# Four residual image layers in one program: layer 0's loop issued in the order of the text, batch statistics moved into layer 2, and the scan's products in bands

## The chip, the cores and the metric

The kernel runs on one core of a Trainium2 chip. The metric is device time in microseconds (us) of one execution; three executions of the kernel before were timed, and the median is used. A core has five instruction queues that run side by side and meet through semaphores: TensorE (PE in the profile; its weight loads are listed apart as PEld), VectorE (DVE), ScalarE (ACT), GpSimd (POOL) and SyncE (SP), which here issues the DMAs. Each queue runs its instructions in the order in which they stand in it, so an instruction that waits holds up what stands behind it.

## What is computed

The input x is 16 images of 64 x 64 pixels and 256 channels in 32-bit floats. Four layers follow one another, each of the form "x plus f(group norm of x)", with 32 groups of 8 channels per image:

```python
# layer 0: linear attention, 8 heads of 32, over the 4096 pixels of an image
q, k, v = split(gn(x) @ Wqkv); q = softmax(q over 32 dims) / sqrt(32); k = softmax(k over pixels)
out = layernorm(((k^T v / 4096) applied to q) @ Wout + bout);  x = x + out
# layer 1: channel gate from mean and max per channel, then two maps of one value per pixel
xc = gn(x) * sigmoid(fc(avg) + fc(max));  m = mean over channels of xc
y  = scan over the 4096 pixels: h = exp(softplus(d*m)*A)*h + softplus(d*m)*m*B(m);  y = sum(h * C)
s  = conv7x7([mean, max over channels of xc]);  x2 = xc*sigmoid(y) + xc*sigmoid(s)
x  = x + relu(batchnorm(x2))               # statistics over all images and pixels
# layers 2 and 3: involution 3x3 and 7x7, each pixel with its own kernel made from its channels
```

Batch norm in layer 1 is the one place where all 16 images meet: its mean and variance need x2 of all of them.

## The kernel before

**Stages.** An image is cut into NCH = 8 chunks of CT = 512 pixels. Activations stand with channels on the 128 partitions, in two halves h. The program is one stage after another: layer 0 (with layer 1's channel gate and maps), layer 1's convolution and scan, layer 1's statistics, layer 2 (which first applies layer 1's end), layer 3. Between stages the activations lie in device memory (x1_d, x2_d, x3_d).

**Layer 0's loop** (from line 566) has LAST = 256 turns and 16 more at its end. An image takes 16 turns: a block of 8 turns for the first 128 output channels of q, k and v (hf = 0), then a block for the others (hf = 1). Turn n, with t = n mod 8, issues work of several stages of several images:

- `attended` projects chunk t of the current block: pq (L280) and pkv (L292) on TensorE, with copies to qa (L284) and ka, va (L301) on ScalarE. Its input xn is normalised (`normalised0`, L166 on VectorE) at the end of the turn before.
- `context` (L318 to L364) belongs to the block before: the maximum of ka by a tree (L311 to L315), a transpose pk (L331), the spreading of the maximum pb (L338), the subtraction (L341) and exponential (L344), the product pctx (L350) of exp(k) with v, and its scaling to cs (L359).
- `weighted` does the softmax of qa: maximum (L387), subtraction on POOL (L375), exponential (L380), sum (L383), reciprocal (L384) and scaling on POOL (L375).
- `output` applies cs to a part of qa: transpose qT (L405), product po (L408), transpose o (L409). PARTS gives the parts of each turn t.
- `projected0`, in the turns of hf = 1, takes the image before: py (L423), bias y (L428), squares (L432) and their sum ss (L433), the scaling of y, transposes pt (L444), yT (L448), the residual addition with maximum (L451), and the store to x1_d.
- `entered` loads the next image's chunk xin and takes statistics (L246); after the eighth, `norm0` makes mean and scale. `gate1` makes layer 1's norm and channel gate after the last projected chunk (av L469, ph L477, pgate L487, gate L491).
- `mapped` takes the image two before: affine of xm (L172, L175), transposes px (L505), and maximum and sum over channels into maps (L509, L510).

The group norms take a power -1/2 on POOL (`inv_sqrt`, L93 and L94, result gn_r). Chains such as `context` are generators: `step()` lets each run to its next yield, and a turn calls it five times (start, twice from `between`, after `entered`, after `mapped`).

In this loop the framework's scheduler decides the order of the instructions in each engine's queue, from the text, dependencies and priorities. The scan and layer 2 stand under `tc.manual_schedule()`: there each queue follows the text.

PSUM buffers set part of the order: py, pkv and px share the tag mm with two buffers, pq, pt and po the tag tr with three, and pk, pb, pctx and the small products one buffer.

**Scan.** The maps of 16 images are turned into r3, whose three kinds of values (softplus d, d*m*m, d*m) are transposed to rows (L726, pr) of 48 partitions, copied (L731), and spread with wrow to 128 partitions of (image, state) by two products pa (L736) of 48 rows each: one for the decay exponent, one for the input. After the exponential a scan instruction (L749) runs over 512 pixels; pys (L760) sums the states. There are 16 steps, 8 chunks by two groups of 8 images.

**Statistics.** For each of 128 tiles of 512 pixels, x1 is loaded (L789), the factor sigmoid(y) + sigmoid(s) is spread over partitions by a product pf (L792) with a one-hot column, VectorE multiplies and sums (L797), and ScalarE squares and sums (L801). Some 20 small VectorE operations make batch norm's scale and shift. The factor, held in SBUF as `held`, is also stored to fac_d.

**Layer 2** begins by loading its constants (17 DMAs on SP), then in each of its first 128 turns reads a tile of x1 and of the factor (`load_layer1`: two DMAs each, the factor broadcast to all partitions), makes z (L970) on VectorE, the relu (L976) on ScalarE and x2 on POOL (L980), and goes on with the involution, whose product pd stands on VectorE (L1102). Its reads of a tile are ordered by image rows: a tile takes 256 pixels from each half of the image.

Of the kernel before, what the change touches and what calls it, by code (L numbers as in the profile page):

```python
# [15 lines left out]
P = 128  # L16
C = 256
# [19 lines left out]
def network(ctx: ExitStack, tc: tile.TileContext, a: dict, out: bass.AP):  # L37
# [142 lines left out]
    with ExitStack() as st:  # L180
# [59 lines left out]
        def entered(i, ch):  # L240

            if ch == 0:
                st0[i] = wk.tile([P, 2, NCH, 6], F32, tag="st0", name="st0")
            xin = loaded.pop(("xin", i, ch))
            for h in range(2):
                nc.vector.bn_stats(st0[i][:, h, ch, :], xin[:, h])  # L246
            if i >= 2:
                stores.extend(halo.pop(0) for _ in range(min(3, len(halo))))
            if ch == NCH - 1:
                chains.append(norm0(i))  # L250
# [8 lines left out]
        normal = {}  # L259

# [57 lines left out]
        def context(i, hf):  # L318
# [4 lines left out]
            t = tree_max(  # L323
                lambda t: [kf[:, 8 * k : 8 * k + 8, :] for k in range(4)]
                + [t.rearrange("p (j e) -> p j e", e=P)],
                lambda t: [(t[:, 0:n], t[:, n : 2 * n]) for n in (512, 256, 128)],
            )
            yield
            yield
            pk = sm.tile([P, CT], F32, tag="sm", name="pk")  # L330
            nc.tensor.transpose(pk[:, 0:P], t[:, 0:P], ident)  # L331
            kmc = small.tile([P, 1], F32, tag="kmc", name="kmc")
            nc.vector.tensor_reduce(kmc, pk[:, 0:P], AX.X, ALU.max)
            diag = wk.tile([P, P], F32, tag="diag", name="diag")
            nc.vector.tensor_scalar(diag, ident, kmc, None, ALU.mult)
            yield
            pb = sm.tile([P, CT], F32, tag="sm", name="pb")
            nc.tensor.matmul(pb[:, 0:P], lhsT=ones, rhs=diag, start=True, stop=True)  # L338
            for jh in range(2):
                part = kf[:, jh * 16 : (jh + 1) * 16, :]  # L340
                nc.vector.tensor_tensor(  # L341
                    part, part, pb[:, 0:P].unsqueeze(1).broadcast_to([P, 16, P]), ALU.subtract
                )
                nc.scalar.activation(part, part, AF.Exp)  # L344
            yield
            yield
            pctx = sm.tile([P, CT], F32, tag="sm", name="pctx")
            for j in range(32):
                for h in range(4):
                    nc.tensor.matmul(  # L350
                        pctx[32 * h : 32 * h + 32, 0 : NB + 1],
                        lhsT=ka[:, j, :, h], rhs=va[:, j, :, h],
                        start=(j == 0), stop=(j == 31),
                    )
            rz = small.tile([P, 1], F32, tag="rz", name="rz")
            nc.vector.reciprocal(rz, pctx[:, NB : NB + 1])

            cs = wk.tile([P, P], F32, tag="cs", name="cs")
            nc.vector.scalar_tensor_tensor(  # L359
                cs.rearrange("p (h e) -> p h e", h=4),  # L360
                pctx[:, 0:NB].unsqueeze(1).broadcast_to([P, 4, NB]), rz,
                hmask.rearrange("p (h e) -> p h e", h=4), ALU.mult, ALU.mult,
            )
            ctx_m[i, hf] = cs  # L364

        def weighted(i, hf):
# [11 lines left out]

            def exponential(k):
# [6 lines left out]
            for k in range(2):  # L386
                nc.vector.tensor_reduce(mq[:, halves[k]], qa[:, halves[k]], AX.X, ALU.max)  # L387
                scaled(k, mq, ALU.subtract)
                yield
            exponential(0)  # L390
            yield
            summed(0)
            exponential(1)
            yield
            scaled(0, mq, ALU.mult)
            summed(1)
            yield
            scaled(1, mq, ALU.mult)
            om[i, hf] = slots.tile([P, P, NB], F32, tag="slot", name="o")
# [13 lines left out]
        def projected0(i, ch):  # L413
# [45 lines left out]
            if ch == NCH - 1:  # L459
                chains.append(gate1(i))  # L460
# [37 lines left out]
        def mapped(i, ch):  # L498

            xc = loaded.pop(("xm", i, ch))  # L500
            affine(xc, xc, i)
            px = mm.tile([P, 4, C], F32, tag="mm", name="px")
# [14 lines left out]
        def jobs(n):  # L517
# [18 lines left out]
            if at(i - 2) and (t >= 2 if hf == 0 else t < 2):  # L536
                todo.append(("xm", i - 2, (t - 2) % NCH))
            if 12 <= d < 16:
# [5 lines left out]
        PARTS = ((), (), (), (0,), (1,), (2, 3), (4, 5), (6, 7))  # L544
        PARTS_LAST = ((), (), (), (0, 1), (2, 3, 4), (5, 6, 7), (), ())

        def loads(n):
            for job in jobs(n):
                if job[0] == "q":
                    load("xn", job[1], job[3])  # L550
                else:
                    load(*job)

        for ch in range(NCH):
# [4 lines left out]
            stores.clear()  # L559
        while chains:  # L560
# [3 lines left out]
        projecting = []  # L564
        for n in range(LAST + 16):
# [5 lines left out]
            loads(n + 1)  # L571
            if t == 0 and 0 <= before[0] < NI:
                chains.append(context(*before))
            if t == 1 and 0 <= before[0] < NI:
                chains.append(weighted(*before))
# [10 lines left out]
            for p in parts[:1]:  # L586
# [6 lines left out]
            def between(dp):  # L593
                step()
                if dp == 0:
                    for p in parts:
                        if p is not parts[0]:
                            next(p)
                    for p in parts:
# [3 lines left out]
                    for p in projecting:  # L603
                        next(p)

# [5 lines left out]
            for job in jobs(n + 1):  # L611
                if job[0] == "q":
                    normalised0(*job[1:])
# [3 lines left out]
            for job in work:  # L617
                if job[0] == "xm":
                    mapped(*job[1:])
            step()  # L620
            if t == NCH - 1 and 0 <= before[0] < NI:
                del qkv[before], ctx_m[before]
                if m >= 3 and m % 2:
                    for k in range(2):
                        om.pop((m // 2 - 1, k), None)

# [4 lines left out]
    with ExitStack() as st:  # L631
# [4 lines left out]
        sm = st.enter_context(tc.tile_pool(name="s_sm", bufs=2, space=PSUM))  # L636

# [6 lines left out]
        bng = sconst("bng", [P, 2], a["bn_gamma"])  # L644
        bnb = sconst("bnb", [P, 2], a["bn_beta"])
# [4 lines left out]
        wrow = sconst("wrow", [3 * NI, NG, 2, P], a["wrow"].rearrange("k (g n s) -> k g n s", g=NG, n=2))  # L650
        wout = sconst("wout", [P, 16], a["wstate"])
        mv2 = sconst("mv2", [P, 2, 2, NI])
# [56 lines left out]
        r3 = sconst("r3", [P, NB, NI, 3])  # L709
        rd, rdmm, rdm = (r3[:, :, :, k].rearrange("p d i -> p i d") for k in range(3))  # L710
        nc.vector.scalar_tensor_tensor(rd, z, 0.0, az, ALU.max, ALU.add)
        nc.vector.tensor_tensor(rdm, rd, m, ALU.mult)
        nc.vector.tensor_tensor(rdmm, rdm, m, ALU.mult)
# [5 lines left out]
        with tc.manual_schedule():  # L719
# [3 lines left out]
            def rowed(ch):  # L723
                pr = tr.tile([P, CT], F32, tag="tr", name="pr")
                for q in range(4):
                    nc.tensor.transpose(  # L726
                        pr[0 : 3 * NI, q * P : (q + 1) * P],
                        r3[:, ch * 4 + q].rearrange("p i k -> p (i k)"), ident,
                    )
                rows[ch] = wk.tile([3 * NI, CT], F32, tag="rows", name="rows", bufs=2)  # L730
                nc.scalar.copy(rows[ch], pr[0 : 3 * NI, :])  # L731

            def decayed(ch, g):
                pa = mm.tile([P, 2, CT], F32, tag="mm", name="pa")
                for k in range(2):
                    nc.tensor.matmul(  # L736
                        pa[:, k], lhsT=wrow[:, g, k, :], rhs=rows[ch], start=True, stop=True
# [42 lines left out]
        facr = fac_d.rearrange("(i c) t -> i (c t)", i=NI)  # L780
# [3 lines left out]
        tot = sconst("tot", [P, 2, 2, NI, NCH])  # L784
        for i in range(NI):
            for ch in range(NCH):
                tk = slice(ch * CT, (ch + 1) * CT)
# [870 lines left out]
```

## Time and profile before

| | |
|---|---|
| median of three executions | 8218.75 us (8206.47 to 8226.33) |
| profiled execution, its own time | 8218.71 us |
| span in its trace | 8216.8 us |
| mean granted TensorE clock | 0.918 |
| layer 0 filling, 0 to 220 | 220 us |
| layer 0's steady loop, 220 to 2880 | 2660 us |
| end of layer 0's loop, 2880 to 3056 | 176 us |
| convolution and scan, 3056 to 3176 | 120 us |
| statistics, 3176 to 3409 | 233 us |
| layer 2's first turns, 3409 to 3554 | 145 us |
| layer 2, 3554 to 5854 | 2300 us |
| layer 3, 5854 to 8217 | 2363 us |

The stages follow one another, so the time is their sum, and a change is worth what it takes from the engine that ends last in its own stage. A busy time is the time in which an engine executed something, summed over the stretch. A row of waits gives the engine and line that waited, the engine, tile and line whose work ended the wait, the total in us, the number of times and the longest. In a row of the timeline, the start, the duration of the group, the engine, the line, the operation with output and inputs, shapes and count follow one another, and in brackets the idle time before it with the work that ended it.

### The profile page before, as it was taken

The numbers are of one execution on the slowest core, as the hardware profiler recorded it, in microseconds if no ns is written. First come the engines' busy times: TensorE is split into PE (matmuls) and PEld (weight loads), VectorE is DVE, ScalarE is ACT, GpSimd is POOL, SyncE is SP. The second block draws the span as 40 slices with busy tenths as digits, with TensorE's granted clock in tenths as the row PEclk, the third lists the DMA queues.
The fourth block names the chain that finished last, engine by engine and source line by source line (L and its number), as shares of the span: only waits on it lengthen the run. The fifth ranks groups of instructions, "written<-read, shape, count | busy, mean of one in ns | idle before, by whom it ended". The sixth has DMA issues, their size and how long they took to land. (4 is left out here: it accounts for less than half of the span.)

```text
span 8216.8 us, 213294 instructions
## 1 busy us (share of the span) xinstructions
PE 6831.6 (83%) x88348; PEld 5191.9 (63%) x88348; DVE 5933.2 (72%) x7071; ACT 4827.7 (59%) x11136; POOL 3044.1 (37%) x2154
## 2 busy tenths in 40 slices
PE   7888888888888867478888888888588888888897
PEld 5666666666666643156666666666477777777776
DVE  6787778787777775679999999999644444444444
ACT  3555555555555544676776767665455555555554
POOL 1222222222222210167888888887411212111112
PEclk9999999999999977798888888888799999999999
DMA  7644444344333334766777777775588888888887
GB/s 225 188 142 138 139 136 141 131 145 144 124 113 118 116 102 151 249 221 231 268 262 261 271 252 267 262 258 200 176 257 258 259 258 256 261 259 257 255 256 245
DMA packets 1079706, 1695.53 MB, mean 206 GB/s; under 512 B 136785, under 2 KB 682914, under 8 KB 1077586
## 3 DMA queue, kind: packets, MB, share of 16 engines
q1 hardware_dynamic: 1078738, 1681.89, 63.1%
q8 instruction: 696, 11.40, 0.6%
q14 instruction: 272, 2.23, 0.1%
HBM read 1234.54 MB, written 469.76 MB: 207 GB/s over the span
## 5 line engine op out<-in xcount | busy, mean ns | idle before, releaser
L1102 DVE TENSOR_TENSOR pd<-xs,pw 128x4608 f32<-128x4608 f32 x256 | 1261.2, 4946 | 1.4 <-ACT xs L1083 1.4
L1376 PE MATMUL pk<-rt,span 64*128 64x176 f32 x12288 | 1177.9, 328 | 52.6 <-issue 47.9
L1386 ACT ACTIVATE wm<-pk,spanb 128x176 f32<-128x176 f32 x2560 | 845.7, 424 | 573.4 <-PE pk L1376 570.3
L1115 POOL TENSOR_TENSOR pd<-pd 128x2048 f32<-128x2048 f32 (+2 forms) x384 | 1071.6, 2791 | 173.1 <-DVE pd L1102 82.7
L1462 POOL TENSOR_TENSOR ex<-ex,rx 128x192 f32<-128x192 f32 (+2 forms) x768 | 436.6, 570 | 1820.6 <-DVE ex L1455 1232.1
L1376 PEld LDWEIGHTS pk<-rt,span 64*128 64x128 f32 x12288 | 967.8, 191 | 132.8 <-issue 75.9
L1455 DVE SCALAR_TENSOR_TENSOR ex<-pa,msk,ex 128x192 f32<-128x192 f32 x704 | 294.3, 418 | 1006.5 <-ACT ex L1454 948.4
L292 PE MATMUL pkv<-wq,xn 128*128 128x256 f32 x4096 | 967.9, 382 | 14.4 <-ACT va L301 14.2
L1442 PE MATMUL pa<-wm,xw 126*32 126x48 f32 x45056 | 758.2, 214 | 220.9 <-issue 206.2
L375 POOL TENSOR_TENSOR qa<-qa,mq 128x1024 f32<-128x1024 f32 x256 | 507.4, 2005 | 1168.8 <-DVE mq L384 503.0
L1079 PE MATMUL pt<-ident,pad 128*128 128x128 f32 x4608 | 760.1, 327 | 214.8 <-ACT xs L1083 207.6
L1391 DVE TENSOR_TENSOR wm<-pk,spanb 128x704 f32<-128x704 f32 x896 | 794.2, 888 | 188.9 <-PE pk L1376 186.3
L292 PEld LDWEIGHTS pkv<-wq,xn 128*128 128x128 f32 x4096 | 771.3, 192 | 227.4 <-issue 101.1
L1442 PEld LDWEIGHTS pa<-wm,xw 126*32 126x32 f32 x45056 | 624.6, 111 | 403.1 <-issue 359.0
L1079 PEld LDWEIGHTS pt<-ident,pad 128*128 128x128 f32 x4608 | 623.6, 168 | 401.4 <-ACT xs L1083 265.5
L1083 ACT COPY xs<-pt 128x512 f32<-128x512 f32 x1152 | 608.0, 587 | 170.1 <-PE pt L1079 167.2
L1273 DVE TENSOR_REDUCE x<-pd 128x512 f32<-128x4608 f32 x128 | 634.0, 4953 | 4.4
L280 PE MATMUL pq<-xn,wq 128*128 128x512 f32 x1024 | 528.2, 631 | 91.2 <-DVE xn L166 74.0
L423 PE MATMUL py<-wo,o 128*128 128x256 f32 x2048 | 525.0, 412 | 31.4 <-DVE maps L510 27.6
L1454 ACT ACTIVATE ex<-pa,msk 128x192 f32<-128x192 f32 x704 | 299.2, 425 | 392.7 <-PE pa L1442 198.5
L423 PEld LDWEIGHTS py<-wo,o 128*128 128x128 f32 x2048 | 487.7, 310 | 63.9 <-issue 38.0
L1033 PE MATMUL px<-x2p,wis 128*128 128x512 f32 x1024 | 467.7, 599 | 12.8 <-DMA x2p<-x_d 8.1
(234 smaller groups left out, 11663.8 us busy)
## 6 DMA issues: line engine op xcount, KB each, us to landing
xw<-strips SPq DMA_DIRECT2D x1408, 256.0 KB
xn<-in_x SPq DMA_DIRECT2D x256, 512.0 KB
x_d<-x SPq DMA_DIRECT2D x256, 512.0 KB
strips<-cen SPq DMA_DIRECT2D x352, 256.0 KB
xin<-in_x SPq DMA_DIRECT2D x128, 512.0 KB
x<-in_x SPq DMA_DIRECT2D x128, 512.0 KB
xm<-x_d SPq DMA_DIRECT2D x128, 512.0 KB
x<-x_d SPq DMA_DIRECT2D x128, 512.0 KB
```

The lines of the kernel that those rows point to most:

```text
L280: nc.tensor.matmul(pq, lhsT=wq[:, h, f0 : f0 + P], rhs=xn[:, h], start=(h == 0), stop=(h == 1),)
L292: nc.tensor.matmul(pkv[:, q], lhsT=xn[:, h, q * P : (q + 1) * P], rhs=wq[:, h, f0 + P : f0 + 384], start=(h == 0), stop=(h == 1),)
L423: nc.tensor.matmul(py[:, q, :], lhsT=om[i, hf][:, :, ch * 4 + q], rhs=wo[:, hf, :], start=(hf == 0), stop=(hf == 1),)
L1079: nc.tensor.transpose(pt[:, k, h * P : (h + 1) * P], lines[:, h, rc * 4 + e + k, 2 * j : 2 * j + P], ident,)
L1083: nc.scalar.copy(xs[:, e : e + 2, j, :], pt)
L1102: nc.vector.tensor_tensor(pd.rearrange("p r (g f) k -> p r g f k", f=16), run, pw.rearrange("p r (g k) -> p r g k", k=9).unsqueeze(3).broa ...
L1115: nc.gpsimd.tensor_tensor(pd[..., 0:n], pd[..., 0:n], pd[..., n : 2 * n], ALU.add)
L1273: nc.vector.tensor_reduce(x3[:, :, P:C], pd1, AX.X, ALU.add)
L1376: nc.tensor.matmul(pkv[:, b, m], lhsT=span[half, first + gg, s0 : s0 + P], rhs=rto[half, o // 4 * 2 + m, :], start=True, stop=True,)
L1386: nc.scalar.activation(dst[:, m // 2, m % 2], pkv[:, m // 2, m % 2], AF.Identity, bias=spanb[:, g0 + m : g0 + m + 1],)
L1391: nc.vector.tensor_tensor(dst, pkv, spanb[:, g0 : g0 + 4].rearrange("p (b m) -> p b m", b=2).unsqueeze(3).broadcast_to([P, 2, 2, NTL]), AL ...
L1442: nc.tensor.matmul(pav[p0 : p0 + 32, :, tj * TC : (tj + 1) * TC].rearrange("c g (w v) -> c g w v", v=2), lhsT=xw[0:TILE_IN, k, tj, 32 * q ...
```

## The change

**Layer 0's loop** comes under `tc.manual_schedule()`, so every queue follows the text, and the text is rearranged. `context` and `weighted` become lists of links, each run at a given step after the chain's start, by the tables CONTEXT and WEIGHTED (a turn has five steps). The chains `norm0` and `gate1` wait in a list `waiting` until turn t = 1 of the next block. PARTS moves to turns 4 to 7, two parts each. The qT of all parts of a turn stands at its start. xn is normalised in `between(0)` and no longer at the end of the turn. The transposes px and the maps come a turn after the affine of xm. x1 is loaded in its own turn and not a turn ahead. xm of the last image but one is taken in turns 2 to 5 behind the last block.

**Statistics** move to the start of layer 2's section, as `batch_norm()`. Images 1 to 15 come first, in 120 tiles; image 0 comes last, in layer 2's own tiles, whose x1 and product z stay in SBUF, so that layer 2's first eight turns load neither x1 nor the factor and make no z. Loads run five tiles ahead in six buffers (four buffers before). `held` is read back from fac_d, behind the constants on SP.

**Scan.** r3 is laid out in bands of 32 partitions: per group of 8 images, one band for d and one for d*m*m and d*m. It is set to zero by POOL first, and filled by six operations and not three. The products pa read 8 and 16 rows at partitions 64g and 64g + 32 instead of 48 rows each.

```diff
@@ layer 0
-                chains.append(norm0(i))
+                waiting.append(norm0(i))
+        def until(links):
+            at = 1
+            for step_no, link in links:
+                while at < step_no:
+                    yield
+                    at += 1
+                link()
-        def context(i, hf):
+        def context(i, hf, at):
...
+            links = [maximum, diagonal, spread] + [
+                lambda jh=jh: exponential(jh) for jh in range(2)
+            ] + [product]
+            return until(zip(at, links))
-        def weighted(i, hf):
+        def weighted(i, hf, at):
...
+            links = []
+            for f in (shifted, exponential, summed, lambda k: scaled(k, mq, ALU.mult)):
+                links += [lambda f=f, k=k: f(k) for k in range(2)]
+            order = sorted(range(8), key=lambda n: at[n])
+            return until([(at[n], links[n]) for n in order] + [(max(at), ended)])
-                chains.append(gate1(i))
+                (waiting if i < NI - 1 else chains).append(gate1(i))
@@ mapped
             affine(xc, xc, i)
+            yield
             px = mm.tile([P, 4, C], F32, tag="mm", name="px")
@@ jobs
-            if at(i - 2) and (t >= 2 if hf == 0 else t < 2):
+            if at(i - 2) and d < 0 and (t >= 2 if hf == 0 else t < 2):
                 todo.append(("xm", i - 2, (t - 2) % NCH))
+            if 2 <= d < 6:
+                todo += [("xm", NI - 2, 2 * d - 4 + k) for k in range(2)]
-        PARTS = ((), (), (), (0,), (1,), (2, 3), (4, 5), (6, 7))
+        PARTS = ((), (), (), (), (0, 1), (2, 3), (4, 5), (6, 7))
+        CONTEXT, CONTEXT_LAST = (1, 5, 14, 14, 15, 19), (1, 3, 4, 4, 4, 7)
+        WEIGHTED, WEIGHTED_LAST = (1, 3, 5, 7, 11, 13, 12, 14), (1, 2, 3, 4, 4, 5, 5, 6)
@@ the loop
+        in_order.enter_context(tc.manual_schedule())
         for n in range(LAST + 16):
...
             loads(n + 1)
+            for job in jobs(n):
+                if job[0] == "x1":
+                    load(*job)
...
+            if t == 1:
+                chains.extend(waiting)
+                waiting.clear()
...
-            for p in parts[:1]:
+            for p in parts:
                 next(p)
             def between(dp):
                 step()
                 if dp == 0:
-                    for p in parts:
-                        if p is not parts[0]:
-                            next(p)
                     for p in parts:
                         next(p, None)
                     for p in old:
                         next(p, None)
                     for p in projecting:
                         next(p)
+                    for job in jobs(n + 1):
+                        if job[0] == "q":
+                            normalised0(*job[1:])
+                    for p in mapping:
+                        next(p, None)
+                    mapping.clear()
...
-            for job in jobs(n + 1):
-                if job[0] == "q":
-                    normalised0(*job[1:])
...
-                    mapped(*job[1:])
+                    mapping.append(mapped(*job[1:]))
+                    next(mapping[-1])
@@ scan
+        r3 = pc.tile([P, NB, 2, 2, 32], F32, tag="r3", name="r3")
+        nc.gpsimd.memset(r3, 0.0)
...
+                    p0 = 64 * g + 32 * k
+                    band = slice(p0, p0 + 8 + 8 * k)
                     nc.tensor.matmul(
-                        pa[:, k], lhsT=wrow[:, g, k, :], rhs=rows[ch], start=True, stop=True
+                        pa[:, k], lhsT=wrow[band], rhs=rows[ch][band], start=True, stop=True
                     )
@@ statistics, now in layer 2
+            nc.sync.dma_start(out=held, in_=fac_d)
+            todo = [(i, ch) for i in range(1, NI) for ch in range(NCH)]
+            todo += [(0, rc) for rc in range(NCH)]
...
+            for k in range(5):
+                begin(k)
+            for k, (i, ch) in enumerate(todo):
+                begin(k + 5)
...
+                for h in range(2):
+                    z = x1[:, h] if i else kept[ch][1][:, h]
+                    at = slice(i * NCH + ch, i * NCH + ch + 1)
+                    nc.vector.scalar_tensor_tensor(
+                        z, x1[:, h], ngm1[:, i, h : h + 1], pf, ALU.add, ALU.mult,
+                        accum_out=tot[:, 0, h, at],
+                    )
+                    sq = z if i else wk.tile([P, CT], F32, tag="sq", name="sq", bufs=1)
+                    nc.scalar.activation(sq, z, AF.Square, accum_out=tot[:, 1, h, at])
@@ layer 2
+            if i:
                 x1, pf = taken("x1"), taken("pf")
...
+            else:
+                x1, zs = (t.rearrange("p h (g t) -> p h g t", g=2) for t in kept.pop(rc))
-            if end:
+            if end and end[0]:
                 load_layer1(*end)
         with tc.manual_schedule():
+            batch_norm()
             loads(0)
```

## Prediction, made before the changed kernel ran

> **What bounds the kernel now.** I read the page's totals, then a table by stage, then one image of layer 0 by blocks, then the waits of TensorE there, then single instructions.
>
> ```profile
> span 8216.8 us, 213294 instructions
> PE 6831.6 (83%) x88348; PEld 5191.9 (63%) x88348; DVE 5933.2 (72%) x7071; ACT 4827.7 (59%) x11136; POOL 3044.1 (37%) x2154
> ```
>
> No engine bounds the whole. The stages, in order: layer 0 filling, its steady loop, its tail, the scan, the statistics, layer 2's start (two rows):
>
> ```profile
> 220.00:2880.00 2660.00, 2314.36 (x16536) 1769.76 (x16535) 2050.61 (x3038) 1539.43 (x2853) 602.06 (x404) 0.95 0.42 137
> 2880.00:3056.00 176.00, 103.38 (x675) 80.85 (x674) 138.82 (x223) 71.94 (x159) 26.71 (x19) 0.72 0.35 116
> 3056.00:3176.00 120.00, 106.76 (x250) 55.76 (x251) 36.11 (x74) 22.26 (x33) 0.00 (x0) 0.54 0.01 2
> 3176.00:3409.00 233.00, 154.94 (x255) 40.81 (x253) 181.29 (x515) 176.87 (x512) 0.00 (x0) 0.93 0.85 280
> 3409.00:3468.00 59.00, 0.00 (x0) 0.00 (x0) 18.38 (x46) 24.29 (x60) 28.74 (x19) 0.50 0.68 186
> 3468.00:3554.00 86.00, 48.54 (x152) 23.92 (x152) 28.98 (x57) 59.34 (x140) 33.80 (x28) 0.79 0.87 293
> ```
>
> Columns: length, then busy PE, PEld, DVE, ACT, POOL, clock, DMA share, GB/s. The reader sees a loop with PE at 87% and DVE at 77%, a scan on PE, statistics and a layer 2 start fed by DMA (0.85, 0.87). Layers 2 and 3 behind 3554 are untouched. The loop holds 231 copies of qa (L284) at 16 per image, so 14.4 images of 184.3 us, of which PE works 160 and DVE 142. One image is two blocks of eight turns; its first rows are the second half of the channels (head, tail), then the first half of the next image (head with one tail turn, three tail turns):
>
> ```profile
> 1317.50:1371.50 54.00, 47.57 (x442) 40.11 (x443) 41.66 (x50) 34.10 (x71) 16.16 (x11) 0.94 0.30 99
> 1371.50:1417.60 46.10, 45.02 (x191) 35.28 (x191) 29.26 (x51) 31.24 (x73) 5.88 (x6) 1.00 0.43 137
> 1417.60:1475.20 57.60, 41.30 (x412) 30.02 (x412) 51.69 (x89) 29.15 (x37) 15.87 (x11) 0.91 0.45 146
> 1475.20:1499.00 23.80, 23.48 (x98) 16.01 (x97) 19.45 (x26) 11.23 (x15) 1.71 (x1) 1.00 0.59 201
> ```
>
> Tails are TensorE's (98%). In the heads it waits, in the third row for a VectorE that is 90% busy. What it waits for in the loop:
>
> ```profile
> PE pq L280 <- DVE xn L166: 74.0, 29, 5.0
> PE pk L331 <- DVE mx L315: 71.5, 28, 3.5
> PE pctx L350 <- DVE isq L93: 45.7, 14, 3.5
> PE py L423 <- DVE maps L510: 25.6, 13, 3.1
> PE px L505 <- ACT xm L172: 24.9, 13, 2.3
> ```
>
> Of 346 us in which PE idles there, these are 241.7, all at places the change moves.
>
> **The loop.** It drops no arithmetic: the same instructions stand in the order of the text, so only waits change. I walked the new order through one image, turn by turn, with durations of the trace.
>
> Second half of the channels, head (54.0). In turn 0 the tree maximum (1.21 + 1.21 + 0.68 + 0.36 + up to 1.99 = 5.3 us of VectorE) stands ahead of y, which frees the PSUM buffer that px and then the second half of pkv need: +3.0. In turn 2 the group norm's chain, now begun in turn 1 behind the softmax's shift, asks POOL for gn_r, and POOL is in two qa subtractions; gn_b waits on VectorE with everything behind it:
>
> ```profile
> 1440.21 3.78 POOL L375 TENSOR_TENSOR qa<-qa,mq 128x1024 f32<-128x1024 f32 x2 [16.07 <-DVE mq L384]
> 1450.86 0.69 POOL L94 TENSOR_TENSOR gn_r<-isq,mhalf 128x2 f32<-128x2 f32 x1 [2.21 <-DVE isq L93]
> ```
>
> That is 3.8 + 0.7 = +4.5. In the text ss (L433) comes straight behind y (L428), with ScalarE's square between, and the x1 addition behind yT:
>
> ```profile
> 1365.48 1.22 DVE L428 TENSOR_TENSOR y<-py,bout 128x1024 f32<-128x1024 f32 x1
> 1369.66 0.17 DVE L433 TENSOR_SCALAR ss<-ss 128x4 f32<-128x4 f32 x1 [2.96 <-ACT sq L432]
> ```
>
> The ss stall is there already; a yT stall in the head is new, +3.4. One output part moves from turn 3 to turn 4, -1.6. The head becomes 63.3. Tail (46.1): PE's 45.0 with small waits are 45.3, and pq waits for xn once, +1.6: 46.9. Block 100.1 -> 110.2.
>
> First half of the channels (57.6 + 23.8 = 81.4). A tail turn is now a chain on VectorE and TensorE (qT, po, o, xn, maps, statistics, affine): 8.15 us against 23.8/3 = 7.9, four of them 32.6. The first four turns lose the pk and pctx waits (71.5/28 = 2.6 and 45.7/14 = 3.3), since diagonal, exponentials and product stand turns apart; PE has 41.3 - 7.8 = 33.5 there, plus 2.0 for xn behind the maximum, plus 8.0 where ph waits for av, av for gn_r, and gn_r on POOL for four qa operations, plus 1.0: 44.5, and 2.4 for VectorE held up beside POOL. Block 79.5.
>
> On that hold-up a rule stands against the trace. The affine of xm (L175) takes 0.55 us alone and 2.14 beside POOL's qa; xn (L166) 0.46 to 0.55 alone, 0.69 on average. The Trainium skill, "SBUF — State Buffer", section "SBUF: two separate sides", calls the shared ports an exclusive lock held for the whole instruction. By it each of 16 qa operations per image (256 of 2.0 us in the span) could stop VectorE fully, 32 us; by the rows, a mean excess of 0.15 to 0.2 on 16 xn, about 3. The rows decide: both orders issue the same 256, and POOL in turns 1 and 2 finds other VectorE work half the time. I take 2.4.
>
> New image 189.7, this one 181.5, the mean one 184.3. This image was shorter than the mean, so I take the gap to the mean, +5: 14.4 x 5 = **+70**. Both ends: below, -97 (four tenths of the 241.7, rival 1); above, +130 (9 per image, if every ss stall of 2.96 also lands on a head).
>
> Costed at nothing: x1's load in its own turn, because the tile is needed only behind yT, some 9 us later (a late one would add its landing to the addition, as the 2.0 us waits of x on yT do today); maps a turn later, nothing reads them before the scan, though px then holds its PSUM buffer in the next turn (counted above); xm of the last image but one in turns 2 to 5 behind the last, inside a tail where VectorE is 79% busy: tail of the loop 0, between -20 and +20. Every load and store stays on SP's queue, which is free half the time (DMA share 0.42).
>
> **The scan.** Two steps and their transposes repeat every 12.65 us on PE, of which pa takes two times 3.78:
>
> ```profile
> 3085.44 3.78 PE L736 MATMUL pa<-rows,wrow 48*128 48x512 f32 x4
> 3089.15 1.89 PE L760 MATMUL pys<-wout,hst 128*128 128x16 f32 x8
> 3090.88 1.03 PE L726 MATMUL pr<-ident,r 128*48 128x128 f32 x4
> ```
>
> The bands put a step's two products in different row groups and PSUM banks. Layer 3's 64-row products (L1376) run 24 in 1.99 us, 0.083 each against 0.217 for a full-height product of 256 columns: about 1.8 times denser. So 3.71 -> 2.05 over 16 steps: -26; none of it if they do not overlap. The rule against it: the Trainium skill, "TensorEngine Tiling (Array Packing)", "Key Properties", has a change of tiling mode drain the array. The nearest row is the weight load of pa at L1442, 359.0 us in 783 waits, 0.46 each: 32 changes would cost +15. But this scan already alternates 48-row and 128-row products, and pys starts at 3089.15 when pa ends at 3089.22. I take 0 for drains and -25. The POOL memset of r3 (about 3.5 us, half of the 7.6 us that twice its size costs elsewhere) lies under the convolution; POOL is idle in this stage. Three DVE operations become six of half size: +0.5, forgotten. The rows copy on 128 partitions costs what 48 do.
>
> **The statistics.** In layer 2's section they stand behind its 17 constant DMAs on SP, which ran from 3413.1 to 3423.3 (10.2 us), and behind a reload of held: first product 14.3 us behind the store against 2.2: +12. The last eight tiles come in 1 KB runs: +4, by 224 against 288 GB/s. Six buffers instead of four: a tile takes 1.82 us, VectorE and ScalarE need 1.34, but DMA is at 0.85: between 0 and -10, I take 0. Kept tiles save layer 2's first eight turns their x1 and pf loads and z. The z of these turns wait for pf's DMA:
>
> ```profile
> 3416.82 0.75 DVE L970 SCALAR_TENSOR_TENSOR z<-x,ngm,pf 128x512 f32<-128x512 f32 x1 [2.63 <-DMA pf<-fac_d]
> 3429.84 0.75 DVE L970 SCALAR_TENSOR_TENSOR z<-x,ngm,pf 128x512 f32<-128x512 f32 x1 [4.21 <-DMA pf<-fac_d]
> ```
>
> From 3409 to 3468 eight turns take 59 us; at ScalarE's pace of 3.5 per turn plus the 5.1 us of batch norm they take about 35: -25, or nothing if x3 and the weights that turn 8 loads are then late. Together **-9**.
>
> **Sum.** +70 - 25 - 9 = +36 against the profiled 8218.71, which is the median of the runs shown (8218.75): **8255**. This kernel's runs let about 0.2%, 16 us, be told from no change.
>
> **Rivals.** (1) Faster. Spreading context over turns takes four tenths of the 241.7 us of PE waits without new ones, -97: 8218.7 - 97 - 34 = 8088, some 8090. For it: PE has 24 us of idle per image and DVE 42, and each moved piece is named in the waits; a POOL that finishes early removes my 4.5 and 8.0. Against: VectorE at 90% in the first-half head, and a strict order has no way round a stall. With -34 from the rest it decides below a period of 185.5 us per image. (2) The side parts give nothing: bands drain or do not overlap, turn 8 of layer 2 waits for its loads. 8219 + 70 = 8289, 8290. For it: the clock of 0.54 in the scan, and DMA at 0.87 right behind. Against: L1376. (3) The change doesn't act, because the loop is held by matrix work that no order shortens: PE's 160 of 184 in a steady chain; then -34 alone, 8185.
>
> **How the numbers follow.** The walk (8220 to 8330 with the side parts as costed) has 0.46, rival 1 has 0.30, rival 2 has 0.15, rival 3 has 0.09. Faster is rival 1, half of rival 3 and a little of the walk's lower edge: 0.37; same 0.07; slower 0.56. The range reaches from rival 1's middle to the walk with +120: 8080 to 8340. The walk alone: 8220 to 8330.
>
> **What would show it.** In the profile after: loop period 187 to 192; POOL named as releaser of gn_b and av; ss waiting on sq in every y turn; pk and pctx waits gone from PE; pa pairs starting together and a scan cycle near 9.4 us; no pf loads in eight turns. The forecast is wrong if the period is under 185.5, or if ss and gn_r stalls fall where PE has its own work.

## The result, and the profile after

The changed kernel takes 8255.89 us (median of four, 8253.33 to 8262.13) against 8220.52 us of the kernel before: 1.0046 times as long, with a 95% interval from 1.0032 to 1.0059. It is slower by 35 us, and the forecast was 8255. The agreement within a microsecond is partly luck: the loop with its tail and the statistics were each off by more than 50 us, in opposite directions. The stages show that. Their rows in the trace after, with the columns as before (length, busy PE, PEld, DVE, ACT, POOL, clock, DMA share, GB/s), are the steady loop, its tail, convolution and scan, the wait for held, the statistics, and layer 2's start:

```profile
220.00:2994.00 2774.00, 2343.90 (x16499) 1770.06 (x16498) 2022.13 (x3063) 1548.67 (x2833) 590.13 (x405) 0.95 0.41 137
2994.00:3197.00 203.00, 106.60 (x674) 85.02 (x674) 150.46 (x241) 73.59 (x161) 29.85 (x20) 0.70 0.28 95
3197.00:3287.00 90.00, 78.15 (x248) 45.83 (x247) 30.56 (x58) 22.21 (x33) 0.00 (x0) 0.56 0.00 0
3287.00:3302.00 15.00, 0.03 (x1) 0.06 (x1) 1.92 (x8) 0.01 (x1) 8.12 (x2) 0.50 0.31 77
3302.00:3476.00 174.00, 145.42 (x272) 42.30 (x272) 169.13 (x503) 168.16 (x501) 0.00 (x0) 0.98 1.04 384
3476.00:3598.00 122.00, 48.07 (x153) 24.30 (x152) 36.46 (x91) 86.98 (x212) 54.38 (x45) 0.71 0.75 242
```

To compare stages, the same events are taken in both traces: the last pq, the first product of the convolution (psc), the store of held, the first pd of layer 2, the first pk of layer 3, and the end of the span.

| stage, between events | before | after | difference | forecast |
|---|---|---|---|---|
| loop, to the last pq | 2884.7 | 2998.2 | +113.5 | +70 |
| tail, to the convolution | 174.7 | 198.5 | +23.8 | 0 |
| convolution and scan, to held's store | 115.0 | 90.3 | -24.7 | -25 |
| statistics and layer 2's start, to pd | 379.3 | 310.7 | -68.6 | -9 |
| layer 2 | 2371.4 | 2371.5 | +0.1 | 0 |
| layer 3 | 2291.7 | 2282.3 | -9.4 | 0 |
| sum | | | +34.7 | +36 |

Layer 3's code is the same in all kernels of this study, and its time from the first pk to the end lay between 2268 and 2306 us in fourteen traces. So -9.4 is no effect. The start of the convolution scatters too: with the loop of before it lay at 3059.4, 3069.3 and 3072.1 in three traces, with the changed loop at 3196.7 and 3204.3. A difference of some 10 us between two single traces shows nothing.

By the two rows of the steady loop (2660.00 us before, 2774.00 after), TensorE is idle in it for 430 us against 346, and busy for 2344 against 2314 on the same products. So some 84 of the 114 us more are waits, and 30 are longer work, as far as modelled matmul ends tell; why the work is longer was not tried.

Of the five waits of TensorE that were read before, pk's and pctx's are gone, and those of pq for xn and of py for maps are halved; px's wait for xm rose from 24.9 to 37.0, and others stand beside it. TensorE's waits in the changed kernel from 220 to 3000 us (engine, line, releaser: total us, times, longest):

```profile
PE ph L498 <- DVE av L490: 99.4, 14, 7.1
PE py L444 <- ACT va L311: 86.7, 42, 4.8
PE px L527 <- ACT xm L172: 37.0, 14, 2.8
PE px L527 <- DVE y L449: 34.6, 13, 2.7
PE pq L290 <- DVE xn L166: 33.9, 29, 1.6
...
PE pt L465 <- ACT qa L294: 22.0, 15, 2.4
```

VectorE's waits in the same stretch, its first line and two further down:

```profile
DVE ss L454 <- ACT sq L453: 260.2, 118, 2.3
...
DVE gn_b L255 <- POOL gn_r L94: 62.7, 14, 4.5
DVE av L490 <- POOL gn_r L94: 36.4, 14, 4.3
```

And the longest of ScalarE's:

```profile
ACT sq L453 <- DVE y L449: 450.3, 118, 7.4
```

The same waits before, from 220 to 2880 us, by the lines of that kernel:

```profile
PE pkv L292 <- ACT va L301: 14.2, 19, 1.3
PE py L423 <- ACT va L301: 2.6, 1, 2.6
...
DVE ss L433 <- ACT sq L432: 179.2, 62, 3.0
...
DVE gn_b L255 <- POOL gn_r L94: 4.7, 14, 0.8
...
ACT sq L432 <- DVE y L428: 123.2, 94, 6.3
```

pk no longer waits for the maximum, and pctx no longer for isq. Instead ph (the channel gate) waits 7.1 us in every image, py waits for the copies of va, and gn_b waits 62.7/14 = 4.5 us. How one leads to the next is seen in one turn of a head of the changed kernel. The timeline of VectorE:

```profile
1399.31 0.16 DVE L255 TENSOR_TENSOR gn_b<-gn_m,gn_r 128x2 f32<-128x2 f32 x1 [4.48 <-POOL gn_r L94]
...
1400.04 1.22 DVE L449 TENSOR_TENSOR y<-py,bout 128x1024 f32<-128x1024 f32 x1
```

That of ScalarE:

```profile
1401.29 0.42 ACT L453 ACTIVATE sq<-y 128x256 f32<-128x256 f32 x1 [6.85 <-DVE y L449]
...
1404.15 1.90 ACT L407 ACTIVATE qa<-qa 128x2048 f32<-128x2048 f32 x1
...
1408.45 0.60 ACT L311 COPY va<-pkv 128x512 f32<-128x512 f32 x1
```

And that of TensorE:

```profile
1401.31 1.09 PE L527 MATMUL px<-ident,xm 128*128 128x128 f32 x8 [2.66 <-DVE y L449]
...
1409.10 5.75 PE L444 MATMUL py<-wo,o 128*128 128x256 f32 x16 [4.75 <-ACT va L311]
```

A tiny operation of two columns waits 4.48 us for POOL. Behind it on VectorE stands y. Behind y, on ScalarE, stand the squares (idle 6.85), and behind them the copy of qa, an exponential of 1.90, yT, xn, and last the copies of ka and va. The next py needs the PSUM buffer that va's copy frees, so TensorE stands still for 2.66 at px and 4.75 at py. In strict queues one late 2-column operation crosses four engines. This is one turn: what each link costs over the whole loop is tested below, and py's wait for va proves to be mostly another matter.

The statistics went the other way. Before, the DMA moved 280 GB/s at a share of 0.85; in the changed kernel's row above it is 384 GB/s at 1.04, and VectorE is busy 169 of 174 us. A share that passes 1 is no measure of how near a ceiling the DMA is.

### The profile page after: what moved, and what is told of

The parts are those of the page before. It is cut to its first block, busy times and chain, and to the rows that moved or that the text cites. A ratio compares the mean times of both kernels' runs of the same rounds, so it can differ in the third digit from the quotient of the medians.

```text
span 8251.5 us, 212941 instructions
## 1 busy us (share of the span) xinstructions
PE 6832.6 (83%) x88364; PEld 5201.1 (63%) x88364; DVE 5865.2 (71%) x7058; ACT 4836.9 (59%) x11136; POOL 3029.6 (37%) x2155
## 4 chain that ended last, share of the span: by engine, by line
PE 44%; DVE 32%; issue 9%; ACT 7%; DMA 5%; POOL 2%; SPq 1%; DVEq 0%; POOLq 0%; ACTq 0%
PE pk L1480 12%; DVE pd L1205 9%; PE pa L1546 8%; DVE x L1377 5%; PE pkv L302 5%; PE pq L290 3%; PE py L444 3%; PE po L429 2%; ACT sq L453 2%; PE pt L1182 2%; PE pr L1447 2%; DVE x L472 2%; DVE mq L403 2%; PE px L1136 1%; POOL qa L398 1%
## 5 line engine op out<-in xcount | busy, mean ns | idle before, releaser
L302 PE MATMUL pkv<-wq,xn 128*128 128x256 f32 x4096 | 994.1, 387 | 0.0
L456 POOL TENSOR_TENSOR rsy<-ss,mhalf 128x4 f32<-128x4 f32 x128 | 132.6, 1036 | 1501.2 <-DVE ss L454 1500.9
L444 PE MATMUL py<-wo,o 128*128 128x256 f32 x2048 | 522.9, 412 | 106.3 <-ACT va L311 86.7
```

The lines of the kernel that those rows point to most:

```text
L302: nc.tensor.matmul(pkv[:, q], lhsT=xn[:, h, q * P : (q + 1) * P], rhs=wq[:, h, f0 + P : f0 + 384], start=(h == 0), stop=(h == 1),)
L444: nc.tensor.matmul(py[:, q, :], lhsT=om[i, hf][:, :, ch * 4 + q], rhs=wo[:, hf, :], start=(hf == 0), stop=(hf == 1),)
```

## The experiments

Each ratio is to the kernel before on the same chip in the same set of runs, with a 95% interval; the changed kernel is 1.0046. The event times are from the profile of each run.

**The side parts alone, and the loop alone.** The first has the diff's parts for scan and statistics, the second its parts for layer 0.

> The loop of before with the statistics in layer 2 and the bands. Theory A, stages add up: before minus 24.7 (scan, 115.0 to 90.3 in the two traces) minus 68.6 (from the store of held to layer 2's first pd, 379.3 to 310.7) minus some 9 in layer 3: 8118 to 8128. Theory B, the gain behind the loop hangs on the new loop (which leaves other data in place, or another clock): less than half of it, above 8165.

> The new loop with the scan and the statistics of before. Theory A: before plus 113 (last pq at 2998 instead of 2885) plus 24 (from there to the convolution), so 8350 to 8360. Theory B: the loop's loss is partly an effect of the other parts, below 8320.

Measured: 8145.78 us, 0.9900 (0.9885 to 0.9914), and 8372.48 us, 1.0174 (1.0156 to 1.0192). On that chip the kernel before takes 8231.35, so the parts are -86 and +141, together +55 where the change as a whole is +35 (1.0032 to 1.0059 of 8220, +26 to +48). The intervals of the two parts are 12 and 15 us wide to each side, so the 20 us between are at the edge of what these runs can tell; within that, the stages add up. The side parts gain a little less than the 91 to 101 us of theory A, and far more than half of it. A kernel with the old loop and the new side parts is faster than the kernel before and the changed one. In its trace the side parts measure 90.5 us from psc to the store and 308.0 from there to pd, as in the changed kernel.

**The order alone.** The changed kernel without the strict order: the text stays rearranged.

```diff
-        in_order = st.enter_context(ExitStack())
-        in_order.enter_context(tc.manual_schedule())
...
-        in_order.close()
```

> The changed kernel, but the scheduler orders the queues of layer 0's loop again; the text stays rearranged. Theory A, the strict order is what costs: last pq back at 2885 within 25, total 8110 to 8150. Theory B, the rearranged text costs (parts two by two, maps a turn later, pieces of context and softmax spread): last pq stays near 2998, total 8230 to 8260. Between: both.

Measured: 8103.20 us, 0.9850 (0.9832 to 0.9867). The last pq is at 2868.3 and the convolution starts at 3026.8, 170 us sooner than in the changed kernel and 33 to 45 sooner than with the loop of before. This is theory A, and more: the rearranged text is no loss, and under the scheduler it is worth some 41 us against the side parts alone (0.9850 against 0.9900). TensorE's largest waits for the steady loop there are far from those of the strict order:

```profile
PE px L527 <- DVE y L449: 58.6, 28, 3.2
...
PE ph L498 <- DVE av L490: 35.9, 13, 2.9
PE pk L344 <- DVE mx L325: 31.8, 15, 4.3
PE py L444 <- ACT va L311: 22.7, 17, 1.5
```

**Six buffers in the statistics.** The kernel before with one number changed.

```diff
-                x1 = wk.tile([P, 2, CT], F32, tag="x1", name="x1", bufs=4)
+                x1 = wk.tile([P, 2, CT], F32, tag="x1", name="x1", bufs=6)
```

> The kernel before with one number changed: six buffers for x1 in the statistics instead of four. Theory A, four buffers leave the DMA waiting for a free buffer: a tile goes from 1.80 us to 1.34 to 1.40, 51 to 59 less, total 8160 to 8170. Theory B, 280 GB/s is what the DMA gives there and the gain in the changed kernel came from the hand order or the layout of tiles: within 15 of before.

Measured: 8174.66 us, 0.9931 (0.9911 to 0.9952), -57. One number in the old kernel gives what the statistics' steady part gives in the changed one. From first to last pf it is 177.6 us for 128 tiles, 1.40 each, against 230.1 before. The stage of this run:

```profile
3184.00:3363.00 179.00, 147.33 (x256) 39.30 (x256) 172.53 (x509) 171.64 (x508) 0.00 (x0) 0.97 0.99 360
```

VectorE now is busy 172.5 of 179 us; the DMA was not at its end before, it waited for a free buffer. Three rows of waits, the first two of the kernel before (3176 to 3409 us; SPq is SyncE's queue, where the loads are issued), the third of this run:

```profile
SPq L789 <- ACT x L801: 170.9, 124, 3.9
DVE x L797 <- DMA x<-x_d: 33.5, 57, 1.8
...
DVE x L797 <- DMA x<-x_d: 2.2, 3, 1.1
```

Before, nearly every load was held at its issue until ScalarE's square had freed a buffer. With six buffers SyncE's queue still waits there (118.2 us), but two loads further ahead, and VectorE hardly waits for data.

**Where the strict order loses: three cuts of the chain.** Four kernels, all in strict order. The first puts the yield ahead of the squares, the second delays the subtractions on POOL, the third has these two edits together, and the fourth starts the norm chains where they are made.

```diff
@@ squares later
             nc.vector.tensor_tensor(y, py, bout.unsqueeze(1).broadcast_to([P, 4, C]), ALU.add)
+            yield
...
             nc.gpsimd.tensor_tensor(rsy, ss, mhalf, ALU.pow)
             yield
-            yield
@@ shift later
-        WEIGHTED, WEIGHTED_LAST = (1, 3, 5, 7, 11, 13, 12, 14), (1, 2, 3, 4, 4, 5, 5, 6)
+        WEIGHTED, WEIGHTED_LAST = (5, 7, 8, 9, 11, 13, 12, 14), (1, 2, 3, 4, 4, 5, 5, 6)
@@ norms at once
-                waiting.append(norm0(i))
+                chains.append(norm0(i))
...
-                (waiting if i < NI - 1 else chains).append(gate1(i))
+                chains.append(gate1(i))
```

> The changed kernel with the squares of y, their sum and the power issued one step later, behind the copy of qa and the transposes of o, and no longer straight behind y. In the changed kernel ScalarE stands 450 us in front of the squares waiting for y, with the copies of qa, ka and va queued behind, and TensorE loses 86.7 us on py waiting for va and 34.6 on px waiting for y; VectorE loses 260 us on ss. Theory A, this chain (y, squares, copies, PSUM buffer, py) is a large part of what the strict order costs: 60 to 110 us faster than the changed kernel. Theory B, the group norms behind POOL are the whole of it and the head's other waits take over: less than 25 faster.

> The changed kernel with one table changed: the softmax's two subtractions on POOL stand four steps later (steps 5 and 7, exponentials at 8 and 9), so that the group norms of turn 1 find POOL free. In the changed kernel TensorE loses 99.4 us on ph waiting for av, and VectorE 62.7 and 36.4 on gn_r. Theory A, POOL's queue is what costs: these three waits fall under 25 each and the kernel gains 50 to 90. Theory B, turn 1 and 2 of a head are full on VectorE anyway, and the wait moves to the subtraction's own users: less than 20 gained, or a loss.

> Both of these edits together. If the two stalls lie one after another on the path, the gains add, and the strict order comes to within 40 of the version that the scheduler orders (8103 in the last runs). If each only uncovers the other, or a third limit (VectorE's 90% in the first-half head), the sum is under six tenths of the two gains.

> The changed kernel with the group norm chains started where they are made, at the end of a block, and not held until turn 1. They then meet TensorE's tail and the maximum of turn 0, and POOL is free of subtractions. Theory A (POOL's queue costs): ph's wait for av falls under 40, 40 to 90 gained. Theory B (the chain costs wherever it stands in a strict order, since VectorE waits at gn_b and av in front of everything else): ph, gn_b and av keep over 100 us of the 198 together, less than 20 gained.

Measured, and the start of the convolution in each trace:

| kernel | us | ratio (interval) | psc starts |
|---|---|---|---|
| changed kernel | 8255.89 | 1.0046 (1.0032 to 1.0059) | 3196.7 |
| squares later | 8157.90 | 0.9937 (0.9916 to 0.9957) | 3103.5 |
| shift later | 8171.71 | 0.9951 (0.9933 to 0.9969) | 3124.8 |
| both | 8197.88 | 0.9979 (0.9969 to 0.9990) | 3145.9 |
| norms at once | 8135.81 | 0.9907 (0.9891 to 0.9924) | 3081.0 |

Each single cut gains 72 to 116 us at the convolution's start. POOL's queue is a cause: with the shift later, VectorE's two waits for gn_r fall from 62.7 to 10.5 and from 36.4 to 0.7, and ph's from 99.4 to 39.0 (under 25 was expected). The gain of 78 us is in theory A's range, though waits for ScalarE grow: pt's for the scaling of y from 15.7 to 89.6, and px's for xm from 37.0 to 63.2. From TensorE's waits with the shift later:

```profile
PE pt L465 <- ACT y L460: 89.6, 16, 6.1
PE py L444 <- ACT va L311: 67.9, 42, 2.2
...
PE px L527 <- ACT xm L172: 63.2, 14, 5.0
PE ph L498 <- DVE av L490: 39.0, 14, 4.2
```

With the norms at once, ph's wait for av and gn_b's for gn_r are not in the lists at all, and VectorE's wait of av for gn_r falls from 36.4 to 10.0: theory A, with a larger gain than its 40 to 90. TensorE's largest waits are now these:

```profile
PE pg L134 <- DVE gn_mv L107: 80.4, 27, 3.3
PE py L444 <- ACT va L311: 73.0, 42, 2.9
PE pq L290 <- ACT xn L165: 35.2, 14, 2.5
```

So py's wait for va (86.7) hangs only in small part on the late norm: it is still 73.0 where gn_b's wait is gone, and 67.9 where it is small.

The squares' place is a cause of its own: ph keeps its 99.4, and 93 us are gained all the same. VectorE's wait at ss falls from 260.2 to 30.8, but the wait at o rises from 88.9 to 242.6, so most of VectorE's idle time only moved. On TensorE, px's wait for y falls from 34.6 to 13.5, py's for va from 86.7 to 68.9, and pt's for qa (22.0) is gone; these are places that ScalarE's copies or y release. From TensorE's waits with the squares later:

```profile
PE py L444 <- ACT va L311: 68.9, 42, 3.4
...
PE px L527 <- DVE y L449: 13.5, 8, 1.7
```

The two edits together gain 51 us at the convolution's start, far under six tenths of the two gains (93 and 72) and less than either, so they do not add; against the shift alone this is at the edge of the intervals. TensorE's waits are not where the sum is lost. In the steady loop it is idle for 370 us with the squares later and for 375 with both, but busy for 2324 and 2359, at a granted clock of 0.96 and 0.94 (the first row is the squares', the second that of both):

```profile
220.00:2914.00 2694.00, 2323.88 (x16517) 1766.65 (x16516) 2015.08 (x3069) 1552.27 (x2842) 604.81 (x405) 0.96 0.42 141
...
220.00:2954.00 2734.00, 2359.09 (x16471) 1797.45 (x16470) 2040.08 (x3054) 1544.87 (x2824) 617.05 (x404) 0.94 0.41 139
```

So 35 of the 40 us between these two are longer work on the same products at a lower clock. It is so in every timed run: over the whole kernel the clock was 0.914 to 0.920 in 16 runs with both edits, and 0.920 to 0.924 in four with the squares alone. What lowered it was not tried.

**Norms at once, with the squares, and with the scheduler.**

> In the strict order, with the norm chains at once and the squares one step later: the two edits that gained 112 and 88 against the changed kernel. Theory A, they take different stalls from the path: at least 150 together, some 0.978 of before, which would beat the scheduled version (0.985). Theory B, as with the squares and the later shift, each edit makes VectorE wait at the transposes of o or the x1 addition in place of the stall removed: no better than the norms alone (0.991).

> The scheduler's order on the new text, with the norm chains at once. If a scheduled queue has gone round POOL already (ph's wait for av is 35.9 us there, not 99.4), this edit is worth little: within 20 of the scheduled version (0.985). If the place in the text counts as much as in the strict order, 60 or more better.

Measured: in strict order with both, 8114.18 us, 0.9888 (0.9867 to 0.9909), 13 us sooner at the convolution than with the norms alone (0.9907), which neither the times nor the traces can tell from nothing. That is theory B: the best strict order tried is still slower than the scheduler's on the same text with the norms held back (0.9850). py's wait for va is 92.1 there (22.7 under the scheduler with the norms held), so this cost of the strict order remains, and what sets it was not found.

With the scheduler and the norms at once: 8020.53 us, 0.9768 (0.9742 to 0.9794), some 67 us better than with the norms held (0.9850), and 52 us at the convolution's start. By the time this is the second expectation, but its reason holds by half only: the same edit gave 116 us at the convolution's start in strict order. The products of the convolution in the trace of the run with the scheduler and the norms at once (line, engine, operation and count, then shortest, median and longest ns, then first and last start in us):

```profile
L727 PE MATMUL psc<-maps,convT x20: 590/601/1190, 2975.0 to 2986.2; 128*128 128x512 f32 x20
```

And in the trace of the strict order with the norms at once:

```profile
L730 PE MATMUL psc<-maps,convT x20: 590/602/1190, 3081.0 to 3090.9; 128*128 128x512 f32 x20
```

| convolution starts at | scheduler | strict order |
|---|---|---|
| norms at once | 2975.0 | 3081.0 |
| norms held until turn 1 | 3026.8 | 3196.7 |
| text of before (norms at once) | 3059.4 | |

So the loop's +137 can be told as three parts, each to some 10 us: the rest of the rearranged text -84, holding the norms +52 under the scheduler, and the strict order +170 on top. The parts hang on the order in which they are taken: with the norms at once the strict order costs 106, and holding the norms costs 116 in strict order. The strict order on the old text was not tried.

**The constants on another queue.** Layer 2's constants are issued from ScalarE's queue, held and the first tiles alone from SP; with the scheduler, and then with the norms at once as well.

```diff
-                nc.sync.dma_start(out=t, in_=src)
+                nc.scalar.dma_start(out=t, in_=src)
```

> The scheduled version with layer 2's 17 constant DMAs issued from ScalarE's queue, so that held and the first x1 tiles are not behind them on SP. In the changed kernel held's load is issued 11.9 us after its store, and the first product 14.9 after. If SP's queue is that wait: product 5 to 7 us after the store, 8 to 10 us less. If the store's own landing and the release of buffers set it: no change there.

> The scheduled order, norm chains at once, and layer 2's constants from ScalarE's queue. The two gains lie in different stages, so they add: 0.9768 less 0.0012 to 0.0015, about 0.9755. If the constants' gain was noise of two chips, 0.9768.

Measured: 8068.21 us, 0.9835 (0.9812 to 0.9858) and 8017.25 us, 0.9763 (0.9738 to 0.9789). Neither can be told from the run without the edit by its time. In the traces the first product of the statistics comes 4.9 to 5.8 us behind the store, not 15.0 to 15.5, so SP's queue was the wait. But from the store to pd it is 304.9 against 310.8, and 307.8 against 310.0 with the norms at once: only 2 to 6 us of the 10 are kept. The tiles then take 179 us from first to last pf, not 173 to 174, most likely because they start while the constants still load (184 to 257 GB/s in the second to fourth of 40 slices of the statistics with the norms held, 202 to 234 with the norms at once, and 370 to 408 in most later ones). The last kernel is the fastest of the study by its median, and not distinguishable from the one with SP's constants.

## Why the prediction was right

The direction, the size of the sum and the place of the loss were forecast: slower, in layer 0's loop, by the waits of a strict order, with the side parts giving part of it back. Its steps:

- The stall of gn_b behind POOL was put at 4.5 us per image and measured 62.7/14 = 4.5; ph behind av and four qa operations was put at 8.0 and measured 7.1. The delayed norm chain is shown as a cause by the norms at once: -116 us at the convolution.
- The step of the loop that was mis-sized is the period: 184.3 + 5 = 189 us per image forecast, 2774/(230/16) = 193.0 measured, just outside the 187 to 192 that was to show it. The walk had py's wait for va at nothing: 86.7/14.4 = 6.0 us per image, where pkv and py together waited 1.2 before. It had y's delay free px's buffer late, and stopped there; ss waiting for the squares was named, but as a cost on VectorE alone, and the run with the squares later shows costs of it on TensorE. Neither the norms nor the squares explain most of py's wait (73.0 and 68.9 without each, 92.1 without both). The walk also kept TensorE's work at 160 us per image, which measured 2344/14.4 = 163.
- Image against image, the walk itself gave 189.7 - 181.5 = +8.2, near the measured +8.7. The step to +5 sets a walked image, made from a short one, against the mean image; this took a third of the difference away (and 14.4 x 5 is 72, not 70). Since the walk lacked the terms above, its +8.2 is luck as well. The steps of the tree maximum add up to 5.45 us, not 5.3; nothing hangs on it.
- On VectorE beside POOL, the walk set the lock that it quotes against the rows. Where an operation meets a POOL operation they agree: here xn begins 0.36 us behind the first of two POOL operations of some 2.0 us, and ends 0.2 us behind it, having taken 1.85 us in place of 0.55. Both rows are of the kernel before:

```profile
1347.96 1.85 DVE L166 TENSOR_SCALAR xn<-xn,gn_m,gn_r 128x512 f32<-128x512 f32 x1 [0.50 <-DMA xn<-in_x]
...
1347.60 3.98 POOL L375 TENSOR_TENSOR qa<-qa,mq 128x1024 f32<-128x1024 f32 x2 [11.69 <-DVE mq L384]
```

  The 32 us took every POOL operation on qa for a full stop of VectorE; the median xn takes 0.55 us and the mean 0.69, so few of them meet one. The 2.4 us of the walk were not tested.
- The tail of the loop was put at 0 and measured +23.8. It loses by the strict order too: it is 158.5 from the last pq to the convolution with the scheduler on the same text.
- The scan was right in its parts: four pa took 2.07 where 3.78 stood, a cycle of two steps 9.33 us (9.4 forecast). One pa by itself takes a median of 1056 ns, and took 1057 before, so they run side by side. In the changed kernel:

```profile
3243.94 2.07 PE L782 MATMUL pa<-rows,wrow 8*128 8x512 f32 x4 [0.68 <-ACT rows L775]
...
3253.27 2.07 PE L782 MATMUL pa<-rows,wrow 8*128 8x512 f32 x4 [0.68 <-ACT rows L775]
3255.27 1.89 PE L806 MATMUL pys<-wout,hst 128*128 128x16 f32 x8
```

  pys starts at 3255.27 and pa ends (by its modelled end) at 3255.34, as in the scan before. The drain at a change of mode, which the prediction priced at +15 from layer 3's weight loads, does not show in this scan.
- In the statistics, two terms held: pf's first product starts 15.0 us behind the store (14.3 forecast; with the store before, so +15 where +12 was forecast, which took off the 2.2 us until the first VectorE product), and layer 2's start is 27 shorter (-25). The failed step is "DMA is at 0.85: between 0 and -10, I take 0". It measured -56 (230.1 to 173.7 from first to last pf, the +4 for the last eight tiles included). A DMA share of 0.85 with VectorE waiting for x1 was read as the DMA's limit. What could have been read there: of the 54.8 us in which VectorE stood still before its product, 33.5 were for a load and 20.3 for ScalarE and TensorE, and SyncE's queue was held 170.9 us at its issues until ScalarE's square had freed a buffer.

So the loop came out 67 us worse than forecast, tail included, and the side parts 59 better. A forecast that got the sum by these two errors is right in its cause and lucky in its size: with the loop as forecast and the statistics as measured, the kernel would have been some 23 us faster than before. Rival 1, the gain from spreading, was true of the text and hidden by the order: under the scheduler the text as it stands takes 8103 us (8090 was rival 1's), and with the norms at once 188 us less than before, of which the side parts are some 86.

## What to carry to other kernels

When a change orders queues by hand, separate the rearranged text from the order before judging either: here the text as it stood was worth some -33 and the order cost +170. In a strict order price each wait by all that stands behind it, through every engine that it feeds, down to the buffer that is freed last; a 2-column operation that stands behind long ones in another engine's queue is the place to look first. And before a DMA share below 1 is taken as a limit, count the buffers in flight.

## What was not expected of the hardware

The same 512 KB loads went from 280 to 360 GB/s in the run where six buffers for four were the only change, and to 384 in the changed kernel, while the share of busy time went from 0.85 to 0.99 and 1.04. And one stage of unchanged code, layer 3, differed by up to 38 us between traces, more than the whole effect that was to be explained.
